# A graph network on one core: picks and adds in pairs, attribute fetches paced one by one, and three loads led by few rows

## The chip, the cores and the metric

The kernel runs on one core of a Trainium2 chip. The metric is the device time of one execution in microseconds (us). Shown are the median of three executions and one execution taken with the hardware profiler, whose lines are quoted in this document.

## The reference

There are 12,500 nodes with 128 features (x) and 200,000 edges, each with a source, a destination, 16 attributes and one of 9 types. The computation has two residual blocks:

```
# block 0: a gated graph layer
messages = segment_sum(x[src] @ W_msg.T + b_msg + embed[type], dst)     # by destination
x1 = layernorm(x + gru_cell(messages, x))
# block 1: three graph layers, edges turned round, each node also its own neighbour
h = x1
for i in range(3):
    ee  = attr @ enc_w[i] + enc_b[i]                   # layer 0 adds ee, layers 1 and 2 append it
    agg = segment_sum([h[dst], ee], src)               # by source
    h   = relu(bn(agg @ w1[i] + b1[i])) @ w2[i] + b2[i]   # relu on all but the last
out = layernorm(x1 + h)
```

What is computed is four passes that each gather 200,000 rows of 128 numbers and sum them by another index, a dense step after each, and once the sums of the edges' attributes by source.

## The kernel before, in words

Nodes are kept in 98 buckets of 128. A first stage, up to about 1264 us of the span, sorts the edges twice on VectorE (once to find each bucket pair's edges, once for the attributes) and makes from the sorted lists, for each pair of buckets, up to 32 slots: which row of the one bucket is wanted, and into which row of the other it is to be added.

Then follow four layers: layer 0 is the gated layer, layers 1 to 3 are the three of block 1. `layer(i, ...)` (line 1485) goes through the 98 target buckets. For each target bucket o:

- *Picks* (line 1615): a table of all rows, X, lies in SBUF as three bf16 parts a row, 384 columns. A matmul of a one-hot `g` (128 x 32) with a bucket's rows (128 x 384) picks 32 rows. Four of these stand side by side in a tile of 128 slots, and three tiles (TG = 3, twelve picks) make a *group*, which fills one PSUM buffer of three banks; `psg` has two such buffers. Layers 0 and 1 have 25 tiles, hence nine groups a bucket, the last of one tile. In layers 2 and 3 only 72 of the 98 source buckets are held in SBUF: 18 tiles, six groups a bucket. The rest comes by `fetch()` (line 1541), an indirect DMA on GpSimd, five tiles a bucket, three buckets ahead.
- *Eviction*: ScalarE copies the group to bf16, `e` (line 1624). In layers 0 and 1, every full group with an even number is shared: ScalarE two tiles (1621), VectorE the third (1622). `e` has four buffers.
- *Adds* (line 1565): a matmul of a one-hot `s` (128 x 128) with each tile of `e` sums the slots into the bank `acc`, of which there is one; line 1570 does the same for fetched tiles. The adds run two groups behind the picks (`add_up_to(2)`), and are left out at group 2 and caught up at group 3.
- *Finish* (lines 1581 to 1583): VectorE adds the three parts of `acc` to `s`, which frees the bank. After every second bucket a generator is put into `work`: `gru` (line 1371) in layer 0, `gin` (line 1425) in the others, which hold the dense step cut into pieces by `yield`. `tick()` runs one piece after each group.
- *One-hots* for the next bucket (`one_hots`, line 1510): VectorE builds `g` (line 1519) from the slots' row `inr`, and `s` in four pieces (line 1524). `inr` comes from DRAM by SP, one row spread to all 128 partitions (line 1507); it has one buffer. In layers 0 and 1 it holds one bucket of 3,136 numbers, in layers 2 and 3 two buckets of 2,304 each, and the next load is issued when the last bucket in it has been used.

The sums of the attributes (`attributes`, line 711) are spread over the sort, layer 0 and layer 1. For each bucket there are 17 indirect DMAs on GpSimd, 128 edges each (line 718), and then `add_up` (line 728): copies and differences on ScalarE and VectorE (738 to 742), a one-hot (743), 17 matmuls (749), three additions (752 to 754). After seven buckets the result is split, transposed and stored to `eaTd` (line 777), from which `gin` loads four buckets at a time (line 1433). `gin` of layer 1 runs the generator on by itself when the sums of its buckets are not there yet (line 1430).

Most engines' instructions are put in order by a scheduler that goes by priorities and buffers. During the sort, VectorE, ScalarE and TensorE keep the order in which the code is written, in the layers GpSimd does. There a tiny copy (`token`, line 1643), which reads `e`, stands ahead of each attribute fetch, so that fetches come in step with the evictions; a buffer of `e` is free again only after that copy. The argument `pace` names the groups of a bucket that get a fetch: seven of nine in layer 0, six in layer 1.

Of the kernel before, what the change touches and what calls it, by code (L numbers as in the profile page):

```python
# [88 lines left out]
def gnn_kernel(ctx: ExitStack, tc: tile.TileContext, x, xx, src, dst, ea, et, w_msg, w_ihT, w_hhT, b_msg,  # L89
# [12 lines left out]
    ovfe = dram("ovfe", (P * NW, EA))  # L102
    x1d = dram("x1", (P, NB, H))

# [3 lines left out]

    inrow = [dram(f"inrow{i}", (NB, n), BF16) for i, n in enumerate((CW, CW))]
    outrow0 = dram("outrow0", (NB, CW), BF16)  # L110
    typerow = dram("typerow", (NB, CW), BF16)
    eaTd = dram("eaT", (E6, NPAD), BF16)

# [597 lines left out]
    def attributes():  # L711


        doing = iter(())
        for b in range(NB):
            at = eap.tile([P, WN, DE], F32, name="eat")
            for t in range(WN):
                G.indirect_dma_start(out=at[:, t, :], out_offset=None, in_=ea,  # L718
                                     in_offset=bass.IndirectOffsetOnAxis(ap=eidcol[:, b, t:t + 1], axis=0))
                if t > 3:  # L720
                    next(doing, None)
                yield
            for _ in doing:
                pass
            doing = add_up(b, at)
        yield from doing

    def add_up(b, at):
# [47 lines left out]
        A.copy(eT, pt[:E6, :XC * P])  # L776
        nc.sync.dma_start(eaTd[:, (b - XC + 1) * P:(b + 1) * P], eT)
        summed.extend(range(b - XC + 1, b + 1))
# [280 lines left out]
    class Slots:  # L1059
# [15 lines left out]
        def decode(self, c):  # L1075
# [19 lines left out]
            field(sl, 11, 127)  # L1095
            nc.sync.dma_start(by_dst(inrow[0])[:, bs, :], as3(sl))
            yield
            field(dl, 4, 127)
            V.scalar_tensor_tensor(dm[:, :m], valid[:, :m], -200.0, dl[:, :m], op0=OP.mult, op1=OP.add)
            field(ty, 0, 15)  # L1100
            nc.sync.dma_start(inrow[1][:, b0 * SL:(b0 + n) * SL], dl[:, :m])
            V.scalar_tensor_tensor(sm[:, :m], valid[:, :m], -200.0, sl[:, :m], op0=OP.mult, op1=OP.add)
# [165 lines left out]
    with by_three():  # L1268
        for _ in spilled:
            next(win, None)  # L1270
            on(range(1))
        on(win)
        for _ in range(2 * WN):
            next(attr)
        later = chain(load_weights(), first_table())

        def some():
            nonlocal done
            for _ in range((3, 3, 3, 2)[done % 4]):
# [12 lines left out]
        for _ in later:  # L1292
            pass
        sorting.append(False)
        stored("A", 1)
        slots = Slots()
        for c in range(3):
            slots.gather(c)
        la = Listed()
        listing = la.mark(2)  # L1300
        next(listing)
        for c in range(2):
            for _ in slots.decode(c):
                next(listing, None)
        for _ in listing:
            pass
# [30 lines left out]
    def layernorm(y, b0, n, final):  # L1337
# [87 lines left out]
    def gin(i, b0, s):  # L1425
        yield
        k4 = b0 % 4
        if k4 == 0:
# [3 lines left out]
            four["eT"] = dq.tile([E6, 4 * P], BF16, name="cT")  # L1432
            nc.sync.dma_start(four["eT"][:, :m * P], eaTd[:, b0 * P:(b0 + m) * P])
            if i == 3:
                four["xx"] = dq.tile([P, 2, 2, 2 * H], F32, name="xx")
                nc.sync.dma_start(four["xx"][:, 0].rearrange("p a (b f) -> p (a b) f", b=2)[:, :m, :], x1d[:, b0:b0 + m, :])
            else:
                four["o"] = dq.tile([P, 4, H], F32, name="n")
# [45 lines left out]

    def layer(i, pace):

# [9 lines left out]
        groups = -(-tiles // TG)  # L1496
        work = []

        inrs = []
# [100 lines left out]
        for o in range(NB):  # L1600
# [6 lines left out]
            for k in range(groups):  # L1607
# [33 lines left out]
                for _ in range(pace.count(k)):  # L1641
                    if _ == 0:
                        G.tensor_copy(token, e[0:1, 0, 0:1])  # L1643
                    next(attr, None)
            for _ in pieces:
                pass
# [6 lines left out]
    for i in range(4):  # L1653
# [55 lines left out]
```

## Time and profile before

| what | us |
|---|---|
| median of three executions (lowest, highest) | 6211.23 (6205.5, 6216.66) |
| the profiled execution | 6211.41 |
| its span, from the first to the last instruction | 6209.6 |
| TensorE, matmuls, busy | 4981.5 |
| VectorE busy | 3730.2 |
| ScalarE busy | 3722.9 |
| GpSimd busy | 3328.5 |
| picks, line 1615, 33,320 instructions | 1954.8 |
| adds, line 1565, 8,428 instructions | 1978.4 |
| evictions by ScalarE, lines 1624 and 1621 | 2260.1 and 627.8 |
| attribute fetches on GpSimd, line 718, 1,666 | 1768.9 |
| row fetches on GpSimd, line 1541, 980 | 974.3 |

The profile names PE for TensorE (PEld for its weight loads), DVE for VectorE, ACT for ScalarE, POOL for GpSimd and SP for SyncE, which issues DMAs. L1615 is line 1615 of the kernel. A row of a group names the line, the engine, the operation, what it writes and reads, and how often. In a timeline a row gives the start in us, the duration, and in brackets how long the engine had been idle and what ended it. The ends of matmuls are modelled, so that neighbours seem to overlap; the distance of their starts is measured. The table of waits gives the waiting engine and line, whom it waited for, the sum in us, how often, and the longest.

The span is also shown in stretches, one row each, with each engine's busy time, TensorE's granted clock, the mean busy share of the sixteen DMA engines, and the GB/s that they moved.

### The profile page before, as it was taken

What the parts mean: (1) busy time and instruction counts of PE and PEld (TensorE: products, weight loads), DVE (VectorE), ACT (ScalarE), POOL (GpSimd) and SP (SyncE); (2) the same over time, 40 slices, a digit from 0 to 9 for tenths busy, and PEclk for the clock granted to TensorE, in tenths of its full rate; (3) what the DMA queues carried; (4) which work ended last, traced back from release to release, by engine and by line L of the source; (5) the groups of instructions that cost most, each with busy time, mean ns of one, the idle gap of its engine ahead of it and who ended that gap; (6) DMA issues with size and microseconds to landing.
All of it is one profiled execution on the core that took longest, in us unless ns stands there. A gap on an engine that the chain in (4) does not pass through costs nothing. (4 is left out here: it accounts for less than half of the span.)

```text
span 6209.6 us, 129682 instructions
## 1 busy us (share of the span) xinstructions
PE 4981.5 (80%) x50669; PEld 2867.1 (46%) x50669; DVE 3730.2 (60%) x9301; ACT 3722.9 (60%) x5300; POOL 3328.5 (54%) x4109
## 2 busy tenths in 40 slices
PE   3872431148888888898899999958999998999999
PEld 3872121124444444443455555534555555555555
DVE  9977777656766766666566656634444443444444
ACT  7770221025665656565677777736777776777776
POOL 1004777356665666665566666663555553655553
PEclk9755555568999999999999999979999999999999
DMA  1001210022222322224222223214444445444443
GB/s 71 22 1 32 84 38 8 11 53 77 82 81 80 96 79 84 81 86 146 83 89 93 91 88 98 89 44 163 143 139 139 139 139 164 145 137 137 136 137 103
DMA packets 278104, 575.34 MB, mean 93 GB/s; under 512 B 74269, under 2 KB 169897, under 8 KB 276835
## 3 DMA queue, kind: packets, MB, share of 16 engines
q1 hardware_dynamic: 158946, 416.84, 19.2%
q0 software_dynamic: 105920, 116.17, 8.1%
q10 hardware_dynamic: 12616, 33.99, 1.6%
q8 instruction: 397, 6.50, 0.4%
q14 instruction: 225, 1.84, 0.1%
HBM read 478.02 MB, written 88.73 MB: 91 GB/s over the span
## 5 line engine op out<-in xcount | busy, mean ns | idle before, releaser
L1624 ACT CAST e<-g 128x1152 bf16<-128x1152 f32 (+1 forms) x2156 | 2260.1, 1061 | 746.7 <-PE g L1615 668.6
L1615 PE MATMUL g<-x,g 128*32 128x384 bf16 x33320 | 1954.8, 335 | 156.1 <-ACT e L1624 80.4
L718 POOL DMA_INDIRECT eat<-in_ea,eidcol x1666 | 1768.9, 1062 | 543.2 <-issue 448.9
L1565 PE MATMUL acc<-e,s 128*128 128x384 bf16 (+3 forms) x8428 | 1978.4, 349 | 89.5 <-DVE s L1583 58.6
L1565 PEld LDWEIGHTS <-s 128*128 128x128 bf16 (+1 forms) x8428 | 1090.2, 155 | 869.8 <-issue 643.8
L1541 POOL DMA_INDIRECT x<-table,rowcol x980 | 974.3, 994 | 918.5 <-PE acc L1570 728.0
L1615 PEld LDWEIGHTS <-g 128*32 128x32 bf16 x33320 | 698.4, 96 | 1077.4 <-issue 851.6
L1621 ACT CAST e<-g 128x768 bf16<-128x768 f32 x784 | 627.8, 801 | 414.8 <-PE g L1615 299.9
L1524 DVE TENSOR_TENSOR s<-iotas,outcol 128x832 bf16<-128x832 bf16 (+1 forms) x1568 | 873.5, 568 | 1.0 <-PE acc L1565 1.0
L1643 POOL COPY token<-e 1x1 bf16<-1x1 bf16 x1274 | 383.2, 301 | 694.9 <-ACT e L1624 444.1
L1622 DVE CAST e<-g 128x384 bf16<-128x384 f32 x784 | 434.4, 554 | 514.9 <-ACT e L1621 508.8
L1519 DVE TENSOR_SCALAR g<-inr,pidx 128x3136 bf16<-128x3136 bf16 (+1 forms) x392 | 370.0, 944 | 573.7 <-PE g L1615 550.5
L557 PE MATMUL acc<-ot,oa 125*98 125x101 bf16 x1600 | 295.8, 359 | 125.9 <-ACT ot L538 85.7
L557 PEld LDWEIGHTS <-oa 125*98 125x98 bf16 x1600 | 291.9, 277 | 129.0 <-issue 82.0
L1581 DVE TENSOR_TENSOR s<-s,acc 128x128 f32<-128x128 f32 x392 | 112.2, 286 | 383.6 <-PE acc L1565 378.4
L538 ACT ACTIVATE ot<-dbb,bias 125x160 bf16<-125x160 bf16 (+2 forms) x1078 | 332.2, 403 | 16.6 <-PE acc L557 15.9
L1570 PE MATMUL acc<-x,s 128*128 128x384 bf16 x980 | 330.8, 338 | 8.7 <-DMA x<-table,rowcol 8.7
L749 PEld LDWEIGHTS <-eoh 128*128 128x128 bf16 x1666 | 117.0, 162 | 307.5 <-DVE eoh L743 240.8
L799 POOL IOTA num<- 98x2176 uint16 x1 | 1.9, 1946 | 459.4 <-DMA sortedB<-keyB 459.4
L738 ACT CAST attr<-eat 128x272 bf16<-128x272 f32 x98 | 43.1, 440 | 324.4 <-DMA eat<-in_ea,eidcol 318.1
L1454 ACT ACTIVATE gates<-d,shift,scale 128x256 f32<-128x256 f32 x294 | 150.0, 560 | 110.7 <-PE d L1452 110.5
L1627 DVE TENSOR_TENSOR e<-iota,typecol 128x30 bf16<-128x30 f32 (+1 forms) x882 | 152.1, 178 | 99.1 <-POOL token L1643 71.6
(421 smaller groups left out, 4817.0 us busy)
## 6 DMA issues: line engine op xcount, KB each, us to landing
inr<-inrow SPq DMA_DIRECT2D x196, 784.0 KB
inr<-inrow SPq DMA_DIRECT2D x98, 1152.0 KB
table<-x SPq DMA_DIRECT2D x72, 384.0 KB
eat<-in_ea,eidcol POOLq DMA_INDIRECT x1666
s<-ovf SPq DMA_DIRECT2D x72, 256.0 KB
x<-table,rowcol POOLq DMA_INDIRECT x980
x<-table ACTq DMA_DIRECT2D x19, 672.0 KB
xx<-in_xx SPq DMA_DIRECT2D x24, 512.0 KB
```

The costliest lines, as they stand in the source:

```text
L538: A.activation(self.ot[j % 2][:, b, :ENDS[j] - c0], dbb[:, c0:ENDS[j]], AF.Sign, bias=self.bias[:, b:b + 1], scale=-1.0)
L557: T.matmul(cps[:NB, :NB + NQ - 1], self.oa[c // HC][:, :, c % HC], self.ot[j % 2][:, :, c - (ENDS[j - 1] if j else 0)], start=(c == 0), st ...
L718: G.indirect_dma_start(out=at[:, t, :], out_offset=None, in_=ea, in_offset=bass.IndirectOffsetOnAxis(ap=eidcol[:, b, t:t + 1], axis=0))
L1519: V.tensor_scalar(g[:, :nb * SL], inr[:, o % per, :nb * SL], pidx, None, op0=OP.is_equal)
L1524: V.tensor_tensor(st[:, f0:f0 + P // 4, :], iotas[:, f0:f0 + P // 4, :tw], outcol[a][:, o, None, c0:c0 + tw].to_broadcast([P, P // 4, tw]) ...
L1541: G.indirect_dma_start(out=place(asked), out_offset=None, in_=tables[i], in_offset=bass.IndirectOffsetOnAxis(ap=rowcol[:, o, p.kept + j:p. ...
L1565: T.matmul(sums[o][:, :wid], st[:m, :, cell + t], e[:m, j, :wid], start=(t == 0), stop=(t == tiles - 1), skip_group_check=True)
L1615: T.matmul(pg[c * SL:(c + 1) * SL, j, :H3], g[:, b * SL:(b + 1) * SL], piece(X, b), start=True, stop=True)
L1621: A.copy(e[:, :2, :H3], pg[:, :2, :H3])
L1622: V.tensor_copy(e[:, 2, :H3], pg[:, 2, :H3])
L1624: A.copy(e[:m, :n, :H3], pg[:m, :n, :H3])
L1643: G.tensor_copy(token, e[0:1, 0, 0:1])
```

## The change

There are four edits.

1. In the layers, an even-numbered group (counted over all buckets) ends after its picks. After an odd one the adds catch up by two groups, and `tick()` runs twice. The picks of two groups so stand in a row, and then the adds of two.
2. `pace` becomes a rate, 7.25 fetches a bucket in layers 0 and 1, spread evenly over the groups; each has its own token. During the sort, `some()` runs 2, 2, 3, 2 steps instead of 3, 3, 3, 2.
3. `attributes()` begins a bucket's `add_up` at the ninth fetch of the next bucket, where it was the fifth, and its pieces take turns with the fetches from there.
4. Three tensors in DRAM get another shape, with an unused row at the end of each block, so that the leading dimensions of their DMAs can't be merged into one: the slots' rows of layers 1 to 3 (stored twice, once for layer 1 in two blocks and once for layers 2 and 3 in seven), x1 (four blocks of 32 partitions) and the attributes' sums (two blocks of 51 rows). The slots' row is spread to `[4, 32]` rows where it was `[128]`, in all layers; in layers 2 and 3 the two buckets' rows now lie next to each other, one run of 9,216 bytes for each partition.

```diff
-    x1d = dram("x1", (P, NB, H))
+    x1d = dram("x1", (4, P // 4 + 1, NB * H))
...
-    inrow = [dram(f"inrow{i}", (NB, n), BF16) for i, n in enumerate((CW, CW))]
+    inrow0 = dram("inrow0", (NB, CW), BF16)
+    inrow = [dram(f"inrow{i}", (h, NB // h + 1, n), BF16) for i, h, n in ((1, 2, CW), (2, 7, IC * SL))]
+
+    def slot_rows(i, o, n):
+        if i == 0:
+            return inrow0[o:o + n, :]
+        t = inrow[i > 1]
+        o, p = divmod(o, NB // t.shape[0])
+        return t[o, p:p + n, :]
...
-    eaTd = dram("eaT", (E6, NPAD), BF16)
+    eaTd = dram("eaT", (2, E6 // 2 + 1, NPAD), BF16)
...
-        doing = iter(())
+        doing, last = iter(()), None
         for b in range(NB):
...
-                if t > 3:
-                    next(doing, None)
+                if t == WN // 2 and last:
+                    for _ in doing:
+                        pass
+                    doing = add_up(*last)
+                next(doing, None)
                 yield
-            for _ in doing:
-                pass
-            doing = add_up(b, at)
+            last = (b, at)
         yield from doing
+        yield from add_up(*last)
...
-        nc.sync.dma_start(eaTd[:, (b - XC + 1) * P:(b + 1) * P], eT)
+        nc.sync.dma_start(eaTd[:, :-1, (b - XC + 1) * P:(b + 1) * P], eT)
...
-            nc.sync.dma_start(inrow[1][:, b0 * SL:(b0 + n) * SL], dl[:, :m])
+            for t in inrow:
+                if b0 * SL < t.shape[2]:
+                    nc.sync.dma_start(t[:, :-1, b0 * SL:(b0 + n) * SL], dl[:, :m])
...
-            for _ in range((3, 3, 3, 2)[done % 4]):
+            for _ in range((2, 2, 3, 2)[done % 4]):
                 next(attr)
...
-        nc.sync.dma_start((out if final else x1d)[:, b0:b0 + n, :], y[:, :n, :])
+        nc.sync.dma_start(out[:, b0:b0 + n, :] if final else x1d[:, :-1, b0 * H:(b0 + n) * H], y[:, :n, :])
...
-            inr = inr.rearrange("p (b c) -> p b c", c=n)
-            nc.sync.dma_start(inr, inrow[a][None, o:o + per, :n].to_broadcast([P, per, n]))
-            inrs.append(inr)
+            rows = slot_rows(i, o, per).rearrange("(x b) c -> x (b c)", x=1)
+            nc.sync.dma_start(inr, rows[:, None, :].to_broadcast([4, P // 4, per * n]))
+            inrs.append(inr.rearrange("p (b c) -> p b c", c=n))
...
-                if k != 2:
-                    add_up_to(2)
                 if k:
                     fetch()
-                tick()
                 next(pieces, None)
...
-                for _ in range(pace.count(k)):
-                    if _ == 0:
-                        G.tensor_copy(token, e[0:1, 0, 0:1])
+                due += rate / groups
+                if due >= 1:
+                    G.tensor_copy(token, e[0:1, 0, 0:1])
                     next(attr, None)
+                    due -= 1
+                if (o * groups + k) % 2 == 0:
+                    continue
+                add_up_to(2)
+                tick()
+                tick()
...
-            layer(i, ((0, 1, 3, 4, 5, 7, 8), (0, 1, 3, 4, 6, 7), (), ())[i])
+            layer(i, (7.25, 7.25, 0, 0)[i])
```

More of the change, by code (lines that the diff above doesn't have):

```diff
@@ L1095, in decode @@
             field(sl, 11, 127)
-            nc.sync.dma_start(by_dst(inrow[0])[:, bs, :], as3(sl))
+            nc.sync.dma_start(by_dst(inrow0)[:, bs, :], as3(sl))
             yield
@@ L1432, in gin @@
             four["eT"] = dq.tile([E6, 4 * P], BF16, name="cT")
-            nc.sync.dma_start(four["eT"][:, :m * P], eaTd[:, b0 * P:(b0 + m) * P])
+            nc.sync.dma_start(four["eT"][:, :m * P], eaTd[:, :-1, b0 * P:(b0 + m) * P])
             if i == 3:
                 four["xx"] = dq.tile([P, 2, 2, 2 * H], F32, name="xx")
-                nc.sync.dma_start(four["xx"][:, 0].rearrange("p a (b f) -> p (a b) f", b=2)[:, :m, :], x1d[:, b0:b0 + m, :])
+                nc.sync.dma_start(four["xx"][:, 0].rearrange("p a (b f) -> p (a b) f", b=2)[:, :m, :], x1d[:, :-1, b0 * H:(b0 + m) * H])
             else:
@@ L1483, in gnn_kernel, with layer @@
     assert PLANS[0].rt == -(-PLANS[0].cells // TG) - 1
-    def layer(i, pace):
+    def layer(i, rate):
         cells_only = i == 0
@@ L1497, in layer @@
         work = []
+        due = 0
         inrs = []
```

## Prediction

> **What bounds the kernel now.** I read the busy shares first, then the waits stage by stage, then the order of instructions in time around each wait. The span is 6209.6 us, the execution 6211.41 us (1.8 us lie outside the span), the median of three runs 6211.23: the sum below is made against 6211.4 and stands for the median as it is.
>
> ```profile
> PE 4981.5 (80%) x50669; PEld 2867.1 (46%) x50669; DVE 3730.2 (60%) x9301; ACT 3722.9 (60%) x5300; POOL 3328.5 (54%) x4109
> ```
>
> TensorE is the busiest, but the stages differ. By the first pick of each layer (line 1615, 9,604 picks in layers 0 and 1, 7,056 in layers 2 and 3) the sorts end at 1264 us, layer 0 lasts to 2909, layer 1 to 4268, layer 2 to 5233, layer 3 to 6196.
>
> *Sort.* From 860 us on, GpSimd fetches attributes back to back (42 in 60 us, 1.43 us each), and VectorE, which sorts, waits for them (waits of 560 to 1264 us: waiter, line, whom, us, times, longest):
>
> ```profile
> DVE eat L739 <- ACT attr L738: 110.2, 15, 30.3
> ```
>
> *Layers 0 and 1* lean on TensorE, with waits of ScalarE on the same fetches (76.1 us in layer 0). Near the end of layer 1 a run of 61 fetches without a pick between them (forced by line 1430, since a last bucket needs all sums) blocks GpSimd from 4096 to 4173 us; tokens wait behind it, evictions wait for the tokens, picks for the evictions (timeline: start, us, work, idle before and whom for):
>
> ```profile
> 4111.73 0.80 PE L1615 MATMUL g<-x,g 128*32 128x384 bf16 x5 [9.24 <-ACT e L1624]
> ...
> 4173.26 0.47 ACT L1624 CAST e<-g 64x384 bf16<-64x384 f32 x1 [18.69 <-POOL token L1643]
> 4173.79 0.51 PE L1615 MATMUL g<-x,g 128*32 128x384 bf16 x4 [17.42 <-ACT e L1624]
> ```
>
> With two idle stretches between (18.79 and 20.06 us before line 749) TensorE loses 65 us there.
>
> *Layers 2 and 3* are TensorE alone, two buckets every 19.4 us. A run of 12 picks takes 0.60 us to the next instruction, the adds 0.81 us (timeline of TensorE):
>
> ```profile
> 4999.92 0.67 PE L1615 MATMUL g<-x,g 128*32 128x384 bf16 x12
> 5000.52 0.71 PE L1565 MATMUL acc<-e,s 128*128 128x384 bf16 x3
> 5001.08 0.33 PE L1570 MATMUL acc<-x,s 128*128 128x384 bf16 x1
> 5001.33 0.67 PE L1615 MATMUL g<-x,g 128*32 128x384 bf16 x12
> ```
>
> Matmuls in the middle of a run follow each other by 0.04 us (picks, four at a time) and 0.16 us (adds): 12 x 0.04 = 0.48 and 4 x 0.16 = 0.64. So each turn from picks to adds costs 0.12 us, each turn back 0.17: 0.29 us a round.
>
> **The change part by part.**
>
> *Fetches in the sort.* The fetches before layer 0 fall from 378 to 315. 63 x 1.43 = 90 us less for GpSimd; VectorE loses 3.7 buckets' sums of 2.9 us (lines 739, 742: 0.44 and 0.45; 743: twice 0.75; 752 to 754: 0.17 each) = 11 us. Afterwards GpSimd needs 281 x 1.43 = 402 us behind the sort's some 480 us of VectorE, and sums start four fetches later, so most of the 110 us go. Bounds: 0 and -121. Not all waits came from a full GpSimd (those around 700 to 800 us did not): I take **-80**.
>
> *Layer 0.* Runs of picks 869 -> 689 by the program's order: 180 x 0.29 = -52. ScalarE's 76 us of waits on fetches mostly go, worth perhaps half. Against it: two ticks in a row put the next step of the GRU right behind the one it needs (lines 1386 to 1391, 76 us of waits now), and tokens rise from 7 to 7.25 a bucket (ScalarE waits 63 us for them now). Bounds -128 and +60; **-60**.
>
> *Layer 1.* With 7.25 fetches a bucket all are done some nine buckets before the end, and the run of 61 is gone: -65. Runs 805 -> 630 would give -50, but GpSimd now bounds it: 641 fetches, token to fetch 0.67 us and fetch 1.0 us,
>
> ```profile
> 3603.08 0.97 POOL L718 DMA_INDIRECT eat<-in_ea,eidcol  x1 [0.16 <-issue]
> 3604.09 0.18 POOL L1643 COPY token<-e 1x1 bf16<-1x1 bf16 x1
> 3604.76 1.02 POOL L718 DMA_INDIRECT eat<-in_ea,eidcol  x1 [0.50 <-issue]
> ```
>
> that is 1.68 x 7.25 = 12.2 us a bucket, where a bucket takes 12.6 now: -0.3 x 88 = -25. Together **-90** (bounds -147 and -40, the latter if the item takes 1.78 us as in the slowest of these rows).
>
> *Layers 2 and 3, turns.* Runs 1065 -> 594. In two buckets five of eleven go; one lies where the next bucket's adds wait for VectorE to empty the sum bank (lines 1581 to 1583) and gives nothing. 4 x 0.29 = 1.15 us of 19.4: a bucket pair would take 18.3.
>
> *Layers 2 and 3, the slots' load.* 1,152 KB for two buckets, into one buffer: issued when the odd bucket's one-hot (line 1519) is built, needed by the even one's, and VectorE works in order, so line 1467, 1469 and the finish stand behind it (timeline of VectorE; line 1519 at 4999.23 released the load at 5000.08):
>
> ```profile
> 5009.15 0.82 DVE L1519 TENSOR_SCALAR g<-inr,pidx 128x2304 bf16<-128x2304 bf16 x1 [3.36 <-PE g L1615]
> 5012.24 0.42 DVE L1467 TENSOR_TENSOR n<-d,wset 128x256 f32<-128x256 f32 x1 [2.27 <-PE d L1462]
> 5012.70 0.29 DVE L1469 TENSOR_SCALAR n<-n 128x256 f32<-128x256 f32 x1
> 5013.65 0.29 DVE L1581 TENSOR_TENSOR s<-s,acc 128x128 f32<-128x128 f32 x1 [0.66 <-PE acc L1565]
> ...
> 5014.85 0.28 DVE L1583 TENSOR_TENSOR s<-s,acc 128x128 f32<-128x128 f32 x1
> ```
>
> Today it lands in some 5 us, all engines busy. No row shows a load led by a dimension of 4; the nearest are the inputs src, dst and et, whose 125 rows kept 0.31 to 0.33 of sixteen engines busy, five of them (stretches: from:to, us, busy times, clock, DMA share, GB/s):
>
> ```profile
> 1.80:9.10 7.30, 0.00 (x0) 0.00 (x0) 0.00 (x0) 1.14 (x1) 7.30 (x5) 1.00 0.31 120
> 9.50:19.50 10.00, 0.00 (x0) 0.00 (x0) 9.37 (x5) 1.53 (x1) 5.10 (x3) 1.00 0.33 134
> 5001.20:5005.10 3.90, 3.65 (x47) 1.89 (x46) 2.25 (x7) 3.31 (x4) 2.11 (x3) 1.00 1.01 342
> 5000.00:5019.40 19.40, 18.71 (x210) 11.02 (x214) 8.53 (x22) 14.74 (x17) 9.84 (x11) 1.00 0.36 113
> ```
>
> 134/(0.33 x 16) = 25.4 GB/s an engine. The last row holds 0.36 x 16 x 19.4 = 112 engine-us, 46 of them this load's (1.18 MB / 25.4), so 4.1 us an engine are other traffic. Bounds of the landing: 5 us, if the load stays spread, and 11.6 + 0.8 + 4.1 = 16.5 us, if four engines move it and all the rest falls beside it. I take four engines, as the words "few DMA engines" say: 1.18 MB / 102 GB/s = 11.6, 0.8 to start, and seven row fetches of 6.1 KB an engine, 0.24 us each, 1.7: 14.1 us. From line 1519 (even) to TensorE's next adds it is 0.8 (its own time) + 0.46 (line 1467 to 1469) + 0.25 + 1.2 (line 1581 to 1583) + 0.34 = 3.05 us, then adds 1.3 and 24 picks 1.2, line 1519 (odd) and the issue 1.2, with 0.2 of semaphores: 6.9 us. So a pair takes 6.9 + 14.1 = 21.0 instead of 19.4: 1.6 x 98 = **+157**, turns included (the load alone decides from 11.4 us on).
>
> [...]
>
> *The rest costs nothing, for these covers.* In layer 1 the slots' load is 784 KB: 7.9 + 0.6 + 1 us against 10.0 us between two one-hots at the tightest, in layer 0 more. Without the cover it would cost as above, 1 us a bucket late. The attribute sums' load (102 KB, two engines) is issued at 5027.92 and read 19 us later; x and ovf likewise, a pair ahead. 18 more stores of slots take 0.33 us each on SP's queue in layer 0, which idles. The first loads of a layer have 12 us (4240.82 to 4252.87): **+6** for three.
>
> Sum: 6211.4 - 80 - 60 - 90 + 157 + 6 = 6144; **I say 6140 us.**
>
> **Rivals.** *A: the slots' load stays hidden*, because the transfer spreads after all or an engine moves more than the early loads show. For it: nothing waits for it today. Against: the order of VectorE's instructions is the same in the changed program, and 11.4 us is all there is. Then -80 - 60 - 90 - 1.15 x 98 + 6 = -337: 5,875 us.
>
> *B (slower): the slots' load lands later still.* The other terms give -224, so it decides from 98 x (6.9 + L - 19.4) = 224, a landing L of 14.8 us, 0.7 us over what I take. At 16 us: 98 x 3.5 = +343, 6,330 us. For it: the same four engines carry a sixteenth each of all else and two of them the attributes' sums; all of it beside the load makes 16.5 us. Against: what is issued after the load on the same queue should stand behind it, and leaves only the row fetches.
>
> *C: ScalarE starves the pairs.* The second group's picks need the bank whose eviction (1.12 us each in layers 2 and 3) follows another. For it: a run of 24 picks takes 1.65 us now, not 1.08, though most of that is the sum bank, which stays. Against: two evictions and their gaps take 2.26 us of a pair's 2.4 to 2.5. Were 0.1 us paid in each of 1,470 pairs, the forecast would become 6,290 us; it is level with before at 0.05 us.
>
> **How the numbers follow.** Forecast 0.50, A 0.15, B 0.20, C 0.15. A measurement of this kernel can tell about 0.2%, 12 us, from no change. The forecast's own range is 6,035 to 6,215: a landing of 13 us takes 108 off, one of 14.8 us adds 70. Of its 0.50 I put 0.46 faster, 0.04 the same; A is faster; B and C are slower, but for 0.01 each. Faster 0.61, same 0.06, slower 0.33. To leave out no more than 0.2 the range goes from 5,900 (upper part of A) to 6,350 (more than half of B, all but the worst of C).
>
> **What would show it.** Right: no run of 61 fetches and no wait of 18 us at the end of layer 1; layer 0 starting near 1,185 us; VectorE's line 1519 waiting some 5 us on the DMA of inr in every other bucket of layers 2 and 3, and a pair of buckets there at 21 us; DMA share near 0.3 while it loads. Wrong: pairs at 18.3 us (A), above 21.8 (B), or line 1615 waiting for ScalarE's line 1624 in most runs (C).

## The result, and the profile after

The changed kernel takes 7,976.68 us (median; 7,961.11 to 7,988.16) where the kernel before takes 6,212.01 (6,205.5 to 6,216.66). The ratio is 1.284, its 95% interval 1.2812 to 1.2868: 1,765 us slower, where some 70 us faster was forecast. The profiled execution has a span of 7,982.6 us.

Where the time lies, by the first pick of each layer (us of the span):

| stage | before | after | difference | forecast |
|---|---|---|---|---|
| sort, up to the first pick | 1,263.9 | 1,179.8 | -84 | -80 |
| layer 0 | 1,645.5 | 1,957.8 | +312 | -60 |
| layer 1 | 1,358.3 | 1,627.5 | +269 | -90 |
| layer 2 | 966.0 | 1,603.9 | +638 | +157 for both |
| layer 3 | 975.9 | 1,613.7 | +638 | (in the row above) |

The profile's page says whose work it now is: first the busy time, in which TensorE falls from 80% to 65% of the span, then the shares of the chain that ended last.

```profile
PE 5153.9 (65%) x50669; PEld 3091.1 (39%) x50669; DVE 3714.2 (47%) x9301; ACT 3671.9 (46%) x5300; POOL 3308.4 (41%) x4255
DMA 39%; PE 8%; DVE 6%; issue 1%; ACT 1%; POOL 0%; SPq 0%; DVEq 0%; ACTq 0%; POOLq 0%
```

By layers (from:to, us, the engines' busy times, granted clock, DMA share, GB/s), all four together:

```profile
1179.80:3137.50 1957.70, 1452.09 (x14351) 736.15 (x14351) 1105.25 (x3922) 947.61 (x1367) 1053.67 (x1539) 0.86 0.30 69
3137.50:4765.00 1627.50, 1280.54 (x13550) 725.50 (x13549) 770.36 (x1797) 880.30 (x1176) 857.78 (x1361) 0.89 0.32 79
4765.00:6368.90 1603.90, 958.14 (x10093) 594.24 (x10092) 409.74 (x1030) 704.30 (x784) 467.05 (x492) 0.79 0.36 86
6368.90:7982.60 1613.70, 956.46 (x10113) 597.97 (x10112) 447.90 (x1305) 677.26 (x703) 466.20 (x490) 0.80 0.35 83
```

In the kernel before, layers 2 and 3 were:

```profile
4267.70:5233.70 966.00, 920.84 (x10093) 541.06 (x10092) 418.42 (x1030) 722.22 (x785) 482.83 (x491) 0.99 0.44 143
5233.70:6209.60 975.90, 921.63 (x10113) 544.32 (x10112) 452.80 (x1305) 696.11 (x703) 491.72 (x490) 0.99 0.43 137
```

So in layers 2 and 3 TensorE was busy for 94 to 95% of the time, and now no compute engine is busy for more than 60%; the DMAs move 83 to 86 GB/s where they moved 137 to 143. DMAs were 1% of the chain that ended last before, and are 39% now.

The sort behaves as forecast. VectorE's waits for ScalarE's copies of fetched attributes (110.2 us before) are down to a third, and layer 0 starts at 1,179.8 us, against "near 1,185":

```profile
DVE eat L750 <- ACT attr L749: 32.5, 4, 15.3
```

Layers 2 and 3 show one wait above all, that of the one-hot (line 1533, which was 1519) for the load of the slots' row. Here is VectorE in layer 2, with the two issues of that load by SP's queue:

```profile
5809.67 0.82 DVE L1533 TENSOR_SCALAR g<-inr,pidx 128x2304 bf16<-128x2304 bf16 x1 [17.34 <-DMA inr<-inrow]
5816.75 0.82 DVE L1533 TENSOR_SCALAR g<-inr,pidx 128x2304 bf16<-128x2304 bf16 x1 [2.46 <-PE g L1629]
5843.20 0.82 DVE L1533 TENSOR_SCALAR g<-inr,pidx 128x2304 bf16<-128x2304 bf16 x1 [19.52 <-DMA inr<-inrow]
```
```profile
5817.60 0.51 SPq L1521 DMA_DIRECT2D inr<-inrow  x1
5851.43 0.54 SPq L1521 DMA_DIRECT2D inr<-inrow  x1
```

From the one-hot of the even bucket to the end of the odd one's, which releases the buffer, 7.9 us pass (5809.67 to 5817.57); the issue takes 0.5; then 25.1 us to the use. In the median the first stretch is 8.3 us in layer 2 and 8.8 in layer 3; it is 23.5 us from the end of the issue to the use, 22.6 to the last packet, and a pair of buckets takes 32.3 us (layer 2) and 32.8 (layer 3). In the kernel before the last packet came after 4.9 us, and the one-hot was built 8.7 us after the issue because TensorE let it.

In layer 1 it is the same wait, in 74 of the 98 buckets (263.4 us together, none before):

```profile
3703.11 1.04 DVE L1533 TENSOR_SCALAR g<-inr,pidx 128x3136 bf16<-128x3136 bf16 x1 [2.68 <-DMA inr<-inrow]
3718.93 1.04 DVE L1533 TENSOR_SCALAR g<-inr,pidx 128x3136 bf16<-128x3136 bf16 x1 [4.25 <-DMA inr<-inrow]
```

One-hot to one-hot is 15.8 us: 1.0 for the one-hot, about 0.5 for the issue, and 14.1 (median) from the issue's end to the use. A bucket took 12.6 us before and could not follow.

In layer 0 this wait is only a part of the 312 us. VectorE and ScalarE there wait more for other transfers too (the fetches of attributes and, on VectorE, of the next slots, `cells`):

```profile
ACT attr L749 <- DMA eat<-in_ea,eidcol: 146.0, 27, 11.6
DVE fi L1103 <- DMA cells<-sortedA,start: 121.3, 18, 10.1
DVE g L1533 <- DMA inr<-inrow: 74.9, 29, 10.0
```

Before, these were 76.1, 5.0 and 0 us. These waits are on two engines and overlap, so they can't be added up to the loss.

### The profile page after: what moved, and what is told of

Same layout as the page of the kernel before. It is cut to its first block, busy times and chain, and to the rows that moved or that the text cites. A ratio compares the mean times of both kernels' runs of the same rounds, so it can differ in the third digit from the quotient of the medians.

```text
span 7982.6 us, 129966 instructions
## 1 busy us (share of the span) xinstructions
PE 5153.9 (65%) x50669; PEld 3091.1 (39%) x50669; DVE 3714.2 (47%) x9301; ACT 3671.9 (46%) x5300; POOL 3308.4 (41%) x4255
## 4 chain that ended last, share of the span: by engine, by line
DMA 39%; PE 8%; DVE 6%; issue 1%; ACT 1%; POOL 0%; SPq 0%; DVEq 0%; ACTq 0%; POOLq 0%
DMA inr<-inrow 37%; PE acc L1579 4%; PE g L1629 3%; DVE g L1533 2%; DMA eat<-in_ea,eidcol 1%; DVE s L1538 1%; PE acc L1584 0%; DVE s L1597 0%; DVE s L1595 0%; DVE s L1596 0%; DVE n L1480 0%; DVE ln_st L1354 0%; DVE y L1490 0%; PE d L1475 0%; ACT e L1638 0%
## 5 line engine op out<-in xcount | busy, mean ns | idle before, releaser
L1638 ACT CAST e<-g 128x1152 bf16<-128x1152 f32 (+1 forms) x2156 | 2226.5, 1063 | 1369.6 <-PE g L1629 1305.2
L1579 PE MATMUL acc<-e,s 128*128 128x384 bf16 (+3 forms) x8428 | 2048.0, 369 | 1238.8 <-DVE s L1597 1198.0
L727 POOL DMA_INDIRECT eat<-in_ea,eidcol x1666 | 1820.9, 1093 | 542.2 <-issue 416.0
L1579 PEld LDWEIGHTS <-s 128*128 128x128 bf16 (+1 forms) x8428 | 1144.7, 154 | 2002.0 <-DVE s L1597 1231.6
L1555 POOL DMA_INDIRECT x<-table,rowcol x980 | 932.9, 952 | 2221.1 <-PE acc L1584 1875.1
L1629 PEld LDWEIGHTS <-g 128*32 128x32 bf16 x33320 | 831.1, 101 | 1435.1 <-issue 1124.1
L1538 DVE TENSOR_TENSOR s<-iotas,outcol 128x832 bf16<-128x832 bf16 (+1 forms) x1568 | 876.3, 568 | 21.9 <-PE acc L1579 21.5
L1654 POOL COPY token<-e 1x1 bf16<-1x1 bf16 x1420 | 348.8, 246 | 1182.6 <-ACT e L1635 778.5
L1584 PE MATMUL acc<-x,s 128*128 128x384 bf16 x980 | 310.4, 349 | 24.5 <-DMA x<-table,rowcol 24.5
L1343 ACT CAST x<-n 128x256 bf16<-128x256 f32 x98 | 39.8, 407 | 564.9 <-DVE n L1482 564.9
L335 DVE TENSOR_TENSOR keyA<-keyA 128x1024 f32<-128x1024 f32 (+1 forms) x178 | 191.3, 1075 | 19.4 <-ACT keyA L351 15.8
```

The costliest lines, as they stand in the source:

```text
L1538: V.tensor_tensor(st[:, f0:f0 + P // 4, :], iotas[:, f0:f0 + P // 4, :tw], outcol[a][:, o, None, c0:c0 + tw].to_broadcast([P, P // 4, tw]) ...
L1555: G.indirect_dma_start(out=place(asked), out_offset=None, in_=tables[i], in_offset=bass.IndirectOffsetOnAxis(ap=rowcol[:, o, p.kept + j:p. ...
L1579: T.matmul(sums[o][:, :wid], st[:m, :, cell + t], e[:m, j, :wid], start=(t == 0), stop=(t == tiles - 1), skip_group_check=True)
L1629: T.matmul(pg[c * SL:(c + 1) * SL, j, :H3], g[:, b * SL:(b + 1) * SL], piece(X, b), start=True, stop=True)
L1638: A.copy(e[:m, :n, :H3], pg[:m, :n, :H3])
```

## The experiments

The runs were made on several chips. The kernel before took 6,211 us on one of them and 6,429 to 6,481 on the others, so that each run is compared with executions of before on its own chip, and stages only between runs on one chip or on chips on which before took the same. The changed kernel itself ran only on a chip where before takes 6,212 us. Where a result below has no interval, it is a single execution.

### Which of the four edits costs

Edit 4's load alone, in both directions. (A load whose outermost dimension has 4 entries is called "led by 4" from here on.) The changed kernel with the slots' row spread straight to 128 rows:

```diff
-            nc.sync.dma_start(inr, rows[:, None, :].to_broadcast([4, P // 4, per * n]))
+            nc.sync.dma_start(inr, rows.to_broadcast([P, per * n]))
```

> The changed kernel with one line undone: the slots' row is spread straight to 128 rows again instead of 4 times 32; the tables in DRAM, x1 and the attributes' sums keep their new shapes, the pairs and the pacing stay. Theory A, the load on four engines is the whole loss: line 1533's waits for it (2,028 us) go, a pair of buckets in layers 2 and 3 falls from 32.5 to about 18.3 us, and the whole ends near my rival A, 5,875 us (5,830 to 5,960). Rival: the pairs of picks and adds, or two ticks in a row, cost something that the late load hides now (evictions starve the picks, GpSimd falls behind): then 6,050 to 6,300 us.

It took 6,507.37 us beside 6,481.28: a ratio of 1.0038 (1.0019 to 1.0057). The wait for the load is all but gone from layers 2 and 3 (4.3 us, where the changed kernel has 1,685.4); the one-hot waits for TensorE again, as before the change (the answer for line 1533; us, times):

```profile
its engine sat idle before it (us, times) until:
  PE g L1629: 300.9, 171
```

So one line of the change holds nearly all of the loss; but what is left is not the 5 to 6% gain of theory A: the rival, that the other edits cost something too, is right at least in part. The other direction, the kernel before with the slots' tables and load of edit 4 alone:

```diff
-    inrow = [dram(f"inrow{i}", (NB, n), BF16) for i, n in enumerate((CW, CW))]
+    inrow0 = dram("inrow0", (NB, CW), BF16)
+    inrow = [dram(f"inrow{i}", (h, NB // h + 1, n), BF16) for i, h, n in ((1, 2, CW), (2, 7, IC * SL))]
...
-            nc.sync.dma_start(inr, inrow[a][None, o:o + per, :n].to_broadcast([P, per, n]))
+            rows = slot_rows(i, o, per).rearrange("(x b) c -> x (b c)", x=1)
+            nc.sync.dma_start(inr, rows[:, None, :].to_broadcast([4, P // 4, per * n]))
```

> The kernel before with the slots' part of edit 4 alone: the rows stored in blocks, each load led by 4. Theory A, the load is the whole loss: a pair in layers 2 and 3 takes the 7.9 us from line 1519 (even) to the issue, 0.5 of issue and 23.5 to the use, some 32 us as in the changed kernel, 98 x 12.6 = +1,235; layers 0 and 1 lose what the changed kernel lost plus what its other edits should have won there, 314 + 60 and 269 + 90 = +730; in all some 8,180 us (7,950 to 8,300), and the sort is as before (layer 0 starts at 1,264 us). Rival: a good part of the loss comes from the pairs and the pacing; then this kernel stays under 7,700 us.

It took 8,243.92 us beside 6,481.28, 1,763 us more (some 1,970 were expected): by itself the load costs what the whole change costs, and on that chip the other edits together come to nearly nothing. Pairs of buckets take 33.1 to 33.6 us in layers 2 and 3, about a microsecond more than with the pairs of edit 1.

Then the other edits one by one, on one chip, with the kernel before profiled on it:

> The kernel before, unchanged, so that its stages can be read on the chip of the other runs of this call. On the chip of e1_spread it took 6,481 us, where the profile of before was taken 6,211. Theory: another granted clock in layers 0 and 1 alone; the pairs of buckets in layers 2 and 3 stay within 2% of 19.4 us, layers 0 and 1 together take up to 230 us more than 3,003 us.

> The kernel before with edit 1 alone: picks of two groups, then adds of two, two ticks in a row; the fetches, the pacing and the loads as before. Spreading the load again left 1.0038 of before with edits 1 to 3, though the sort is some 80 to 100 us shorter, so something in the layers costs that much. Theory P, the pairs cost it (two evictions must end before the next two picks, a step of the GRU directly behind the one it needs): 50 to 160 us slower than before, most of it in layers 0 and 1, layers 2 and 3 within 20 us of before. Theory F, the pacing costs it: the pairs alone are 40 to 120 us faster than before.

```diff
-                if k != 2:
-                    add_up_to(2)
...
-                tick()
...
+                if (o * groups + k) % 2 == 0:
+                    continue
+                add_up_to(2)
+                tick()
+                tick()
```

> The kernel before with edits 2 and 3 alone: fetches one by one at 7.25 a bucket, 2, 2, 3, 2 steps in the sort, the sums half a bucket later; groups and ticks as before. Theory P: the sort is 70 to 110 us shorter, the run of 61 fetches at the end of layer 1 is gone (-65), so 90 to 180 us faster than before. Theory F: what the sort wins is lost in layers 0 and 1, where 7.25 fetches fall where 7 and 6 did: within 40 us of before.

```diff
-                for _ in range(pace.count(k)):
-                    if _ == 0:
-                        G.tensor_copy(token, e[0:1, 0, 0:1])
-                    next(attr, None)
+                due += rate / groups
+                if due >= 1:
+                    G.tensor_copy(token, e[0:1, 0, 0:1])
+                    next(attr, None)
+                    due -= 1
...
-            for _ in range((3, 3, 3, 2)[done % 4]):
+            for _ in range((2, 2, 3, 2)[done % 4]):
```

(with `attributes()` as changed), and edits 1 to 3 together:

> The changed kernel with all of edit 4 undone: the slots' rows, x1 and the attributes' sums as before, edits 1 to 3 as they are. If the layouts of x1 and of the attributes' sums cost nothing, as I predicted, it stands where e1_spread stands: 0.995 to 1.010 of before. If they cost (theory X), it is 0.97 to 0.99.

| us of the span | sort | layer 0 | layer 1 | layer 2 | layer 3 | ratio to before |
|---|---|---|---|---|---|---|
| before_again | 1,288.2 | 1,758.1 | 1,383.7 | 997.9 | 1,011.4 | |
| pairs_only | 1,289.5 | 1,782.0 | 1,425.1 | 977.2 | 984.4 | 1.0041 (1.0029 to 1.0054) |
| pacing_only | 1,180.9 | 1,759.0 | 1,402.3 | 998.8 | 1,013.8 | 0.9882 (0.9866 to 0.9899) |
| without_edit4 | 1,184.8 | 1,805.2 | 1,463.5 | 977.5 | 984.7 | 0.9977 (0.9968 to 0.9987) |

The pacing's gain is the sort's, 107 us; layer 1 loses 19. The pairs win 48 us in layers 2 and 3 and lose 65 in layers 0 and 1. So theory P has the sign and the place of the pairs' loss right, but not the size (26 us slower in the median instead of 50 to 160, and layers 2 and 3 win more than 20); pacing_only, with 74 us off the median, falls short of the 90 to 180 that it expected. without_edit4 fell into the range of "the layouts cost nothing"; the runs on one chip below show that they do cost something. A part of the pairs' loss in layer 1 stands in the waits of TensorE's picks there (us, times, longest), first before_again, then pairs_only:

```profile
PE g L1615 <- DVE e L1622: 16.7, 18, 1.8
PE g L1615 <- ACT e L1624: 45.6, 58, 17.4
```
```profile
PE g L1615 <- DVE e L1622: 64.0, 74, 2.4
PE g L1615 <- ACT e L1624: 30.0, 45, 7.8
```

The two groups of a pair want both banks. With adds in between, VectorE's third of a shared eviction had time; without them the picks wait 47 us more for it, and 16 less for ScalarE's. The stop of TensorE near the end of the layer, before line 749, also grew, from 46 to 64 us. In all TensorE idles 52 us more and is busy 11 us less, which makes the 41 us that the layer lost; so the turns saved there are worth far less than in layers 2 and 3, where it is busy 51 us less in each. Why that is so was not tested. before_again shows where the chip's 230 us are: 113 in layer 0 and 25 in each of the sort and layer 1, but layers 2 and 3 lose 32 and 35, though the median pair takes 19.5 us in layer 2, within the 2% that was expected. In layer 2 some 25 of the 32 us lie in one pair that takes 53.8 us, where the longest took 29.3.

On a chip where before takes 6,211 us the same edits 1 to 3 are worth more, and the table layouts of edit 4 could be put beside them:

> The changed kernel without edit 4 again, beside the next run on one chip. 0.9977 of before on the other chip; 0.994 to 1.001 here.

> Edits 1 to 3, and of edit 4 the layouts of x1 (four blocks) and of the attributes' sums (two blocks) alone; the slots' rows as before. With the slots' load spread, all of the new tables and edits 1 to 3 gave 1.0038 of before, without the new tables 0.9977, on two chips. If these two layouts cost the 0.6%, this run is 30 to 60 us slower than the run beside it, in layers 0 and 1; if they cost nothing, as I predicted, it is within 15 us of it.

```diff
-    x1d = dram("x1", (P, NB, H))
+    x1d = dram("x1", (4, P // 4 + 1, NB * H))
...
-    eaTd = dram("eaT", (E6, NPAD), BF16)
+    eaTd = dram("eaT", (2, E6 // 2 + 1, NPAD), BF16)
```

| us | median | ratio to before | sort | layer 0 | layer 1 | layer 2 | layer 3 |
|---|---|---|---|---|---|---|---|
| edits123_again | 6,028.49 | 0.9704 (0.9687 to 0.9720) | 1,174.4 | 1,654.3 | 1,348.3 | 915.1 | 931.0 |
| x1_sums_few | 6,065.18 | 0.9756 (0.9733 to 0.9779) | 1,177.5 | 1,687.0 | 1,357.1 | 915.4 | 933.1 |

0.9704 lies outside the 0.994 to 1.001 that was expected: how much the three edits win depends on the chip. Here a pair of buckets takes 18.31 us in the median of layer 2 and 18.44 in layer 3, where the working with 0.29 us a turn gave 18.25; without_edit4 has 19.16 in layer 2, beside 19.52 in before_again. This is TensorE in layer 2 of edits123_again, two groups' picks, then two groups' adds; in the whole pair it waits only twice, both times for VectorE's finish (line 1586), here at line 1444 and once more for 0.50 us at line 1568:

```profile
4299.87 1.16 PE L1618 MATMUL g<-x,g 128*32 128x384 bf16 x24
4300.96 0.72 PE L1568 MATMUL acc<-e,s 128*128 128x384 bf16 x3
...
4302.42 1.16 PE L1618 MATMUL g<-x,g 128*32 128x384 bf16 x24
...
4305.08 1.16 PE L1618 MATMUL g<-x,g 128*32 128x384 bf16 x24
4306.76 0.33 PE L1444 MATMUL d<-ident,s 128*128 128x128 f32 x1 [0.52 <-DVE s L1586]
4306.93 1.14 PE L1568 MATMUL acc<-e,s 128*128 128x384 bf16 x6
```

The layouts of x1 and of the sums cost 37 us. A third chip told which:

> Edits 1 to 3 without edit 4 once more, so that the next run stands beside it on one chip. 0.970 of before on one chip, 0.998 on another: 0.968 to 1.000 here.

> Edits 1 to 3 and the layout of x1 (four blocks of 32 partitions) alone. x1 and the attributes' sums together cost 37 us, 33 of them in layer 0, where x1 is stored 49 times (four engines for 128 rows of 1 KB) and the sums only seven times. So if the store of x1 is what costs, this run is 25 to 40 us slower than the one beside it; if the sums cost (their loads and stores on two engines), it is within 10 us of it.

Without them 6,415.95 us (ratio 0.9976, 0.9965 to 0.9988), with x1's alone 6,447.86 (1.0030, 1.0015 to 1.0044): 32 us, so it is x1 for the most part. (The expectation miscounted: layer 0 stores x1 twelve times, 512 KB each, and once 128 KB.) What waits for these stores was not found in the waits; that stays open.

### Why the load lands so late

First, whether the row fetches beside it do it. They are left out here, but for those that fill the ring:

```diff
-                if k:
-                    fetch()
...
-        for _ in range(rb * rt):
+        for _ in range(rb * XC if rt else 0):
             fetch()
```

> The changed kernel without the row fetches of layers 2 and 3 but for the first 21 that fill the ring (the sums so use stale rows; this part of the computation is left out), everything else as it is. Theory T1, the load is late since the row fetches go through the same four engines: their packets leave the engines, the load lands in 12 to 14.5 us after its issue instead of 23.5, a pair falls from 32.5 to 21 to 23 us and the whole to 6,850 to 7,050 us. Theory T2, four engines that read one row are slow by themselves (a packet of 9,216 bytes took 0.55 us in the middle where 0.35 is the least): the landing stays at 19 us or more and the whole above 7,550 us.

And whether the four engines hinder each other at one place of DRAM; the row is stored four times, a copy for each leading row of the load:

```diff
+    copies = dram("inrow2", (4, 7, NB // 7 + 1, IC * SL), BF16)
...
+            rows = rows.rearrange("(x b) c -> x (b c)", x=1) if i < 2 else rows.rearrange("x b c -> x (b c)")
             nc.sync.dma_start(inr, rows[:, None, :].to_broadcast([4, P // 4, per * n]))
```

> The changed kernel with the slots' rows of layers 2 and 3 stored four times, so that each of the four leading rows of the load reads a copy of its own (54 more stores of slots in layer 0). Theory T1 (the row fetches beside it) and a theory that the writes are slow: no change, 23.5 us of landing and 7,950 to 8,020 us. Theory T2a, the engines get in each other's way because all read the same place of DRAM: the packets come near 0.35 us, landing 12.5 to 16 us, the whole 6,850 to 7,300 us.

They took 7,818.64 and 7,953.95 us. The load, which takes 21.7 us from its first packet to its last in the changed kernel, got 2.7 us shorter without row fetches and 1.5 with four copies: T2 for the first, a little of T2a for the second. (These two ran on the chip of e2_before_four, whose load took 21.5 us.) Then the number of engines:

```diff
-            nc.sync.dma_start(inr, rows[:, None, :].to_broadcast([4, P // 4, per * n]))
+            nc.sync.dma_start(inr, rows[:, None, :].to_broadcast([8, P // 8, per * n]))
```

> The changed kernel with the slots' load led by 8 instead of 4. If an engine moved 25.4 GB/s beside the row fetches, as I predicted, the load would land 8 to 9 us after the issue's end and be hidden: pairs of buckets at 18.6 to 19.3 us. If a packet of 9,216 bytes takes the 0.56 us that it took on four engines even without row fetches (16 of them an engine, 9 us, and 1 to start, 1 to 2 of row fetches), the landing is 11 to 13 us and a pair takes 20 to 21.5 us. By either the whole is 1.00 to 1.04 of before.

6,783.78 us beside 6,211.07, worse than either theory: 14.6 us from the issue's end to the use, pairs of 23.3 us. Last, another source, with and without row fetches, and 16 leading rows (`[16, P // 16, per * n]` in the same line):

```diff
-            nc.sync.dma_start(inr, rows[:, None, :].to_broadcast([4, P // 4, per * n]))
+            if i < 2:
+                nc.sync.dma_start(inr, rows[:, None, :].to_broadcast([4, P // 4, per * n]))
+            else:
+                nc.sync.dma_start(inr, tables[i][:4 * 33 * 12, :].rearrange("(x p q) c -> x p (q c)", x=4, q=12)[:, :-1, :])
```

> The changed kernel, but in layers 2 and 3 the load into inr reads 128 different runs of 9,216 bytes (from the table of rows, four blocks of 32, so four leading rows as before) instead of one run 128 times. What it brings is not the slots' rows, so the one-hots and sums of these layers are not those of the reference; bytes, engines, destination and order are the same. If reading one place over and over makes the packets slow (four copies took the landing from 21.7 to 20.2 us), they come near 0.35 us, the load lands in 12.5 to 16 us, a pair of buckets takes 21 to 25 us. If the source doesn't matter, 21 to 23 us of landing and 32 us a pair.

> The same load from 128 different runs, and also without the row fetches of layers 2 and 3 but the first 21 (left out as in e4_no_row_fetch, where the load took 19.0 us). If the source is the cause: 11.5 to 13.5 us, what 25.4 GB/s an engine gives, and a pair at 19 to 21.5 us. If not, 18 to 20 us again.

> The changed kernel with the slots' load led by 16 rows of 8 instead of 4 of 32. Spread straight to 128 rows the load took 4.65 us (0.445 us a packet); led by 8 rows it took 12.7 (0.70 a packet), led by 4 21.7 (0.576). If only the number of engines counts, 16 lead to 4.5 to 5.5 us and pairs of 18.3 to 19.3. If a leading dimension slows every engine as it does with 8, 6.5 to 8 us, still hidden: the same pairs.

They took 8,046.18, 7,709.94 and 6,581.19 us beside 6,479.12. The load from other runs is as slow as expected if the source doesn't matter; led by 16 it takes 6.0 us, between the two expectations. All forms of the load in layers 2 and 3, 1.18 MB each, from the DMA packets in the traces (a packet is 9,216 bytes, 4,608 in the kernel before; GB/s is 1.18 MB by the load's duration; the least a packet of 9,216 bytes took is 0.345 us; pairs are medians of layer 2):

| form of the load | mean packet, us | first to last packet, us | GB/s | pair of buckets, us |
|---|---|---|---|---|
| before: 128 rows, two runs each | 0.206 | 4.2 | 282 | 19.4 |
| 128 rows (e1_spread) | 0.445 | 4.7 | 254 | 19.3 |
| led by 16 | 0.614 | 6.0 | 198 | 18.9 |
| led by 8 | 0.700 | 12.7 | 93 | 23.3 |
| led by 4 (after) | 0.576 | 21.7 | 54 | 32.3 |
| led by 4, four copies | 0.519 | 20.2 | 58 | 30.4 |
| led by 4, 128 other runs | 0.547 | 21.4 | 55 | 31.4 |
| led by 4, no row fetches | 0.564 | 19.0 | 62 | 29.9 |
| led by 4, other runs, no row fetches | 0.516 | 17.8 | 66 | 27.8 |

VectorE's wait for the load, in layers 2 and 3 together, goes with it; three answers for the one-hot's line (us, times), after, without row fetches, and led by 8:

```profile
  DMA inr<-inrow: 1685.4, 95
```
```profile
  DMA inr<-inrow: 1400.0, 95
```
```profile
  DMA inr<-inrow: 771.3, 87
```

Neither the source nor the row fetches are the main cause: with both taken away the load still needs 17.8 us, 66 GB/s or 16.5 GB/s an engine, where I had 25.4. Nor is it other traffic: all other packets during a load add up to 91 us of packet time in the changed kernel, and to 6 us in that run. That the leading rows limit how many engines work fits the packets: led by 4 at most 6 packets of the load are under way at once in most loads, led by 8 at most 10 or 11, led by 16 and spread over 128 rows 18 to 19. So does what follows on SP's queue: in layer 2 of the changed kernel the DMA `s<-ovf` of 512 packets is issued at 5822.78, behind the load issued at 5817.60, whose last packet ends at 5842.0; 384 of the 512 start at 5824.0 to 5826.1, beside the load, and 128, a quarter, only from 5840.3 on, and the same 384 and 128 are found at 44 loads of layers 2 and 3. But the row of 16 says that there is more. As many of its packets are under way at once as of the spread load's, it reads the same bytes, and its packets still take 0.614 us instead of 0.445; what differs in the code is that the 128 rows stand in 16 blocks of 8. And the packets led by 4 fall into groups: without row fetches 20% take less than 0.37 us, near the least, and 26% take 0.68 to 0.73 us, about twice that.

Why a packet takes longer in the loads led by 4, 8 and 16 rows (0.516 to 0.700 us) than in the spread one (0.445) was not shown: no run changed the order of the partitions and left the rest as it is.

### A faster kernel

The runs above say what to keep: the sort's pacing, the pairs in layers 2 and 3 alone, no edit 4, and fetches moved from layer 1, which they hold up, to layer 0.

```diff
+                if i < 2 and k != 2:
+                    add_up_to(2)
...
+                if i < 2:
+                    tick()
...
-                if (o * groups + k) % 2 == 0:
+                if i < 2 or (o * groups + k) % 2 == 0:
                     continue
                 add_up_to(2)
                 tick()
                 tick()
...
-            layer(i, (7.25, 7.25, 0, 0)[i])
+            layer(i, (8.25, 5.75, 0, 0)[i])
```

(against edits 1 to 3 without edit 4)

> Another kernel: before with edits 2 and 3, the pairs of edit 1 in layers 2 and 3 alone, no edit 4, and 8.25 fetches a bucket in layer 0, 5.75 in layer 1 instead of 7.25 in both. The pacing alone gave 0.988; the pairs won 48 us in layers 2 and 3 and lost 65 in layers 0 and 1. In layer 1 7.25 fetches bind a bucket pair at 27.7 us where before took 25.4, so 5.75 should give 25.3 without the stop at the end: 1,402 to 1,270 us. In layer 0 a fetch takes some 1.9 us of GpSimd, 8.25 make 15.8 us of a bucket's 17.9: up to +30. In all 0.96 to 0.975 of before; 0.985 or more if layer 0 can't take the fetches.

> The kernel of b1_rates with 6 fetches a bucket in layer 1 instead of 5.75. There one pair at the end of layer 1 still took 50.9 us where others took 25, since its sums were not ready; with 6 they are done two buckets earlier: 15 to 25 us faster than b1_rates (0.965), that is 0.960 to 0.963 of before on a chip like that one, 0.965 to 0.975 on the others.

b1_rates took 5,995.42 us, 0.9648 of before (0.9631 to 0.9664), on the chip of edits123_again: layer 1 fell to 1,308 us instead of the 1,270 expected; 26 of the 38 us are one pair at its end that still took 50.9 us. Edits 1 to 3 took 6,028 there. With 6 fetches (b2_rates, on the chip of edits123_third) that pair takes 31.4 us, and the whole is 0.9763 (0.9743 to 0.9783), against 0.9976 for edits 1 to 3 there; the expectation for such a chip was 0.965 to 0.975. Both are faster than the kernel before and than the changed one.

## Why the prediction was wrong, point by point

- **The slots' load in layers 2 and 3 (+157; measured +638 in each layer).** This step failed, by a term's size. The mechanism was right: line 1519's successor waits for `inr` in every other bucket, and a pair is what lies between the use and the next issue plus the landing. That sum holds: 8.3 + 0.5 + 23.5 = 32.3 in layer 2 and 8.8 + 0.5 + 23.6 = 32.9 in layer 3, against 32.3 and 32.8 measured; I had 6.9 for the first part, issue included. The term that was mis-sized is the landing, **14.1 us forecast, 23.5 measured**, and in it 25.4 GB/s an engine, from early loads with five engines and nothing beside them. The nearer row was this load itself: spread over 16 engines (a DMA share of 1.01 from 5001.20 to 5005.10) it moved 282 GB/s in the profile of before, 17.6 an engine. By that rate four engines need 16.8 us, and with 0.8 for the start and 1.7 for the row fetches 19.3, past the 16.5 that I took for the upper bound. That bound was made of the wrong rate and so bounded nothing. Even this row would have fallen 4 us short: the load moved 54 GB/s, 13.6 an engine. That there are four engines, no row of before showed; the packets of `s<-ovf` after, 128 of 512 of which run only as the load ends, fit it.
- **Rival B** was what happened: the landing is past its 14.8 us. Its price (6,330 us at 16 us) came from the same rate, and the -224 us of the other terms, from which its 14.8 was worked out, became -91 in edits123_again, where the load is spread (sort -90, layer 0 +9, layer 1 -10).
- **"In layer 1 the slots' load ... against 10.0 us", priced at nothing; in layer 0 "more".** Failed for the same reason. In layer 1 the load takes 12.1 us instead of 7.9, and the use follows 14.1 after the issue, so there was no cover. Between x1_sums_few and the changed kernel, which differ by the slots' tables and load and ran on chips where before takes the same, layer 0 loses 271 us and layer 1 270: where the prediction has "1 us a bucket late", it was 2.8. In layer 0 VectorE waited only 75 us for this load. What I left out altogether is that other transfers slowed with the load: between the same two runs VectorE's wait for `cells` grew from 51.1 to 121.3 us and ScalarE's for the attributes from 88.3 to 146.0.
- **x1 and the sums, priced at nothing**: 37 us; x1's layout alone cost 32 on another chip. **Layer starts +6**: not told apart.
- **Sort (-80)**: right, -84 to -107.
- **Layers 2 and 3, turns (18.3 us a pair)**: right, 18.31, when the load is spread and the chip is like the first; 19.15 on others, where the gain is a third of that. The two layers win 96 us of the 113 booked (98 x 1.15); their pairs got 1.08 us shorter.
- **Layer 0 (-60)**: wrong, +9 on the chip like the first, +47 on another. On the latter the pairs alone cost 24 and the pacing alone 1. ScalarE's waits on fetches, half of whose 76 us I booked as gain, stayed at 74.9 in edits123_again, and VectorE's wait for `cells`, which I didn't look at, grew from 5.0 to 52.7. It is 3.6 with the pairs alone and 20.4 with the pacing alone, so it seems to come with the pacing; no run tested that.
- **Layer 1 (-90)**: -10 and +80. One term was also miscalculated: between 12.2 and 12.6 us a bucket lie 0.4 us, not 0.3, which makes -35 instead of -25. The run of 61 fetches did go: the pair that held it took 99.4 us before, 24 to 30 at the end of layer 1 in edits123_again. But the other pairs together took some 60 us longer, in part because the picks wait for VectorE's evictions: 48.0 us, where it was 7.1 before. I had looked for that (rival C) in layers 2 and 3, where ScalarE evicts alone, and not in layers 0 and 1, where VectorE shares it and is busier.
- **Rival A** (5,875 us if the load stays hidden): without edit 4 the edits give 6,028, and with the layouts of x1 and the sums 6,065; the 150 us between are layers 0 and 1.

## What to carry to other kernels

Price a transfer that is confined to fewer engines by its own rate in the trace when spread (here 17.6 GB/s an engine), not by the best rate that an engine shows elsewhere (25.4), and expect that even this rate may be missed (13.6), and that what is fetched beside it may slow too (packets of 512 bytes from 0.07 us to 0.19). A load with one buffer is hidden only until its landing reaches the gap between its release and its use; from there each microsecond is paid once per use, here 98 times a layer or 49. And two groups of the same kind in a row saved turns where one engine alone empties their banks, and lost in layers 0 and 1, where the picks then waited more for the evictions.

## What the runs showed of the hardware

- The slots' load led by 8 rows was slower per packet than led by 4 (0.700 us against 0.576 for 9,216 bytes), and led by 16 rows slower than spread over 128 (0.614 against 0.445).
- Other transfers were slower beside the load led by four rows: in layers 0 and 1 packets of 512 bytes of the attribute fetches took 0.19 us in the mean while the slots' load ran, 0.05 in the kernel before and 0.07 in x1_sums_few, and ScalarE's waits on fetches in these two layers grew from 159.1 us to 273.0.
- One program took 6,211 us on one chip and 6,429 to 6,481 on others, with a mean granted clock of 0.888 and 0.873 to 0.879 (1 to 2% lower, where the time is 3.5 to 4.3% longer), and the same three edits were worth 3.0% on the one and 0.2% on two of the others.
